# The last stage of a graph kernel: the addition of y moved from GpSimd to VectorE, in an order written out by hand

## The chip, the cores and the metric

The kernel runs on one core of one Trainium2 chip. A core has engines that run side by side, each with its own queue of instructions that it takes in order: TensorE (PE, matrix products into PSUM), VectorE (DVE), ScalarE (ACT), GpSimd (POOL), and SyncE (SP), whose queue issues most of the transfers between HBM and the on-chip memory SBUF. [...] The metric is the time of one execution on the device in microseconds (us), the median of several runs.

## The reference

A graph with 6250 nodes of 256 features and 100,000 edges, sorted by target node, goes through three relational layers, a residual layer norm, an attention of a special kind, and another residual layer norm:

```
for l in range(3):
    msg = (x @ W_rel[l, r])[edge_type, src]            # r = edge_type, 8 of them
    x = relu(segment_sum(msg, dst) + x @ W_root[l] + bias[l])
y = layernorm(x_in + x)
xt = (y @ weight).reshape(n, 4, 64)                    # 4 heads of 64
alpha = softmax(leaky_relu(<xt[src], attn_l> + <xt[dst], attn_r>), over heads)
tmp[i] = sum over h of alpha[i, h] * xt[dst[i], h]      # the first n edges only
out = layernorm(y + tmp repeated over the 4 heads)
```

The sum `tmp` of row i belongs to edge i, not to node i. As the edges are sorted by target, the targets of the first 6250 edges are a few nodes with small numbers (below 32 here), so `xt[dst]` takes rows of a small table.

## The kernel before, in words

The 6250 nodes make 49 tiles of 128 rows (`NT`), the last with 106. Function `fast` runs everything: the tables of the edges (`tables`), the three layers (`layer`), and then `attention`. The layers are by far the longest part, and the change leaves their code alone; they run under `tc.manual_schedule()`, which keeps the instructions of each engine in the order in which the program gives them. `attention` is called outside of it: there the framework puts the instructions of each engine into an order of its own, by its own estimates. In both cases the framework adds the waits that data and buffers ask for.

The last layer writes y, tile by tile, to HBM. `attention` (lines 889 to 1034) then works in these steps:

1. Tables: `ohd` (a one-hot of each edge's target, 32 wide), `mask`, and `v` and `v3`, the logits of the few nodes concerned; `yp` is cleared on GpSimd (L929). TensorE makes the logits (L938) and `xt` (L952), the transformed features of the small nodes, with the four heads stacked along the partitions.
2. Scores (L961 to L983): the 49 tiles are cut into nine parts of `G` = 6 tiles, the last of them with a single tile (tile 48, 106 rows). For each part TensorE selects logits with one-hot matrices into a PSUM buffer of pool `ps_1`, VectorE multiplies with the mask (`sel`), sums it (`s1`, `s2`), adds the two and adds `ga`, giving `sc`.
3. Softmax over the heads, for all tiles at once (`softmax`, L861 to L867): the weights `a`.
4. `bn` (L990 to L994): for each part VectorE multiplies `ohd` with `a`: for each edge 4 x 32 numbers that are a head's weight at the target's place and zero elsewhere.
5. The parts (L996 to L1033), one after the other in program order. SP loads six tiles of y (`yg`, 768 KB, four buffers). TensorE turns `bn` (L1005, PSUM pool `ps_2`, two buffers), ScalarE copies it out (`bt`, L1007), TensorE multiplies it with `xt` (L1010, `po` in pool `ps_3`), ScalarE copies the product out (`td`, L1012), GpSimd adds y to it, repeating the 64 numbers for the four heads (`z`, L1014, two buffers). Then the layer norm: VectorE takes statistics (L1024, L1025), ScalarE the root (`rs`, L1026), VectorE the reciprocal and the offset (`rs` L1027, `nb` L1028), ScalarE applies them tile by tile (`o`, L1032), and SP stores `o` (`store`: L853 for full tiles, L856 for the 106 rows of the last tile).

The parts run in the order of `parts[1:] + parts[:1]`: the single tile is the eighth, and the last is the part with tiles 0 to 5. The exponential and the root are in different tables of ScalarE, so a table is loaded before the exponential and another before the first root (both appear in the trace as ACT_TABLE_LOAD).

Of the kernel before, what the change touches and what calls it, by code (L numbers as in the profile page):

```python
# [20 lines left out]
P = 128  # L21
# [137 lines left out]
def fast(tc, const, pl, x, xs, src, dst, edge_type, w_rel, w_root, bias, weight,  # L159
# [10 lines left out]
    with ExitStack() as top:  # L170
        tab = top.enter_context(tc.tile_pool(name="tab", bufs=1))
        ident = tab.tile([P, P], F32, name="ident")
        idx = tab.tile([P, CH * P], I32, name="idx")
        key = tab.tile([P, CH * P], F32, name="key")
        pos = tab.tile([1, CH * P], I32, name="pos")
        iota_p = tab.tile([P, 1], F32, name="iota_p")
        eps = tab.tile([P, 1], F32, name="eps")
        bias_b = tab.tile([P, L, D], F32, name="bias_b")
        w1x = tab.tile([P, KC, D + 2 * H], F32, name="w1x")
        altab = tab.tile([P, NT, H], F32, name="altab")  # L180
        al3 = tab.tile([P, 3, NT, H], BF16, name="al3")
# [12 lines left out]

        dram = top.enter_context(tc.tile_pool(name="lanes", bufs=1, space=DRAM))
        lane = dram.tile([NT * P], I32, name="lane")
        with tc.tile_pool(name="ps_p", bufs=2, space=PSUM) as ps_p:
            tables(tc, pl, ps_p, src, dst, edge_type, ident, idx, key, pos, iota, iota_p,
                   lane, hk, hl, hif, dt, flag, R, H)
        y = dram.tile([NT * P, D], F32, name="y")  # L200

        with ExitStack() as s:
            wp = s.enter_context(tc.tile_pool(name="wp", bufs=1))
            sp = s.enter_context(tc.tile_pool(name="sp", bufs=1))
            mp = s.enter_context(tc.tile_pool(name="mp", bufs=8))
# [12 lines left out]
            nc.vector.memset(eps, EPS)  # L218
            for t in S:
                nc.scalar.memzero(t)  # L220
            nc.sync.dma_start(bias_b, bias.rearrange("l d -> (l d)").partition_broadcast(P))
            fold_weights(tc, mp, w1x, weight, attn_l, attn_r)

            def load_w(l):
                wr = wp.tile([P, KC, R, D], F32, name="wr")
                wo = wp.tile([P, KC, D], F32, name="wo")
                for k in range(KC):
                    nc.scalar.dma_start(
                        wr[:, k], w_rel[l, :, k * P:(k + 1) * P, :].rearrange("r p e -> p r e"))
                    nc.scalar.dma_start(wo[:, k], w_root[l, k * P:(k + 1) * P, :])  # L230
                return wr, wo

            groups = pl.order()

            ready = {}
            for i, (f, g) in enumerate(groups):
                for j in pl.reach(g):
                    ready[f, j] = i

            with tc.manual_schedule():  # L240
                for l in range(L):
                    wr, wo = load_w(l)
                    opn = layer(
                        tc, pl, l, l == L - 1, groups, ready, S, hold, A, hk, hl, idx, key, pos,
                        iota, ident, wr, wo, bias_b, x, xs, eps, w1x, altab, y,
                        (al3, ga, hif, yT0, lane, dst, iota_p),
                        mp, op, xp, hp, ps_w, ps_d, ps_t, H)

        attention(tc, pl, opn, A, al3, ga, hif, dt, yT0, iota, ident, eps, w1x, altab, y, out, H)


def tables(tc, pl, ps_t, src, dst, edge_type, ident, idx, key, pos, iota, iota_p, lane, hk, hl,
# [634 lines left out]
def attention(tc, pl, opn, A, al3, ga, hif, dt, yT0, iota, ident, eps, w1x, altab, y, out, H):  # L887
# [13 lines left out]
    with ExitStack() as s:  # L901
        q1 = s.enter_context(tc.tile_pool(name="q1", bufs=1))
        q2 = s.enter_context(tc.tile_pool(name="q2", bufs=2))
        q3 = s.enter_context(tc.tile_pool(name="q3", bufs=4))
        ps_1 = s.enter_context(tc.tile_pool(name="ps_1", bufs=3, space=PSUM))
        ps_2 = s.enter_context(tc.tile_pool(name="ps_2", bufs=2, space=PSUM))
        ps_3 = s.enter_context(tc.tile_pool(name="ps_3", bufs=2, space=PSUM))
        low, high = halves(A)

        parts = [range(a, min(a + G, NT)) for a in range(0, NT, G)]  # L910
        parts = parts[1:] + parts[:1]

        def rows_of(js):
            t = q3.tile([P, G, D], F32, name="yg")
            nc.sync.dma_start(t[:, :len(js)], y[js[0] * P:(js[-1] + 1) * P, :].rearrange(
                "(t p) d -> p t d", p=P))
            return t


        ohd = q1.tile([P, NT, DB], F32, name="ohd")  # L920
# [36 lines left out]


        sc = q1.tile([P, NT, H], F32, name="sc")
        C = NL * 3 * H  # L960
        for js in parts:  # L961
            g, e = len(js), slice(js[0], js[-1] + 1)
            pg = ps_1.tile([P, 512], F32, name="p1")
            for u, t in enumerate(js):
# [7 lines left out]
            nc.vector.tensor_tensor(  # L972
                sel[:, :g], pg[:, :g * C].rearrange("p (t n q) -> p t n q", t=g, n=NL),
                mask[:, e].unsqueeze(3).to_broadcast([P, g, NL, 3 * H]), ALU.mult)
            s1 = q2.tile([P, G, H], F32, name="s1")
            s2 = q2.tile([P, G, H], F32, name="s2")
            nc.vector.tensor_reduce(s1[:, :g], sel[:, :g].rearrange("p t n (c h) -> p t h (n c)", h=H),
                                    AX.X, ALU.add)
            nc.vector.tensor_reduce(
                s2[:, :g], pg[:, G * C:G * C + g * 3 * H].rearrange("p (t c h) -> p t h c", t=g, h=H),  # L980
                AX.X, ALU.add)
            nc.vector.tensor_tensor(s1[:, :g], s1[:, :g], s2[:, :g], ALU.add)
            nc.vector.tensor_tensor(sc[:, e], s1[:, :g], ga[:, e], ALU.add)  # L983
        a = q1.tile([P, NT, H], F32, name="a")
        m = q1.tile([P, NT], F32, name="m")
        softmax(nc, a, sc, m, NT, H)


        bn = q1.tile([P, NT, H, DB], F32, name="bn")
        for js in parts:  # L990
            g, e = len(js), slice(js[0], js[-1] + 1)
            nc.vector.tensor_tensor(  # L992
                bn[:, e], ohd[:, e].unsqueeze(2).to_broadcast([P, g, H, DB]),
                a[:, e].unsqueeze(3).to_broadcast([P, g, H, DB]), ALU.mult)  # L994

        for js in parts:  # L996
            g, e = len(js), slice(js[0], js[-1] + 1)
            yg = rows_of(js)

            bt = q2.tile([P, G, P], F32, name="bt")  # L1000
            for u0 in range(0, g, 4):
                n = min(4, g - u0)
# [5 lines left out]
            po = ps_3.tile([P, 512], F32, name="p3")  # L1008
            for u in range(g):
                nc.tensor.matmul(po[:, u * DH:(u + 1) * DH], bt[:, u], xt, start=True, stop=True)  # L1010
            td = q2.tile([P, G, DH], F32, name="td")
            nc.scalar.copy(td[:, :g].rearrange("p g d -> p (g d)"), po[:, :g * DH])  # L1012
            z = q2.tile([P, G, D], F32, name="z")
            nc.gpsimd.tensor_tensor(  # L1014
                z[:, :g].rearrange("p g (h d) -> p g h d", h=H),
                yg[:, :g].rearrange("p g (h d) -> p g h d", h=H),
                td[:, :g].unsqueeze(2).to_broadcast([P, g, H, DH]), ALU.add)

            st = q2.tile([P, G, 6], F32, name="st")
            mv = q2.tile([P, G, 2], F32, name="mv")  # L1020
            rs = q2.tile([P, G], F32, name="rs")
            nb = q2.tile([P, G], F32, name="nb")
            for t in range(g):
                nc.vector.bn_stats(st[:, t], z[:, t])  # L1024
                nc.vector.bn_aggr(mv[:, t], st[:, t])  # L1025
            nc.scalar.activation(rs[:, :g], mv[:, :g, 1], AF.Sqrt, bias=eps)  # L1026
            nc.vector.reciprocal(rs[:, :g], rs[:, :g])  # L1027
            nc.vector.scalar_tensor_tensor(nb[:, :g], mv[:, :g, 0], -1.0, rs[:, :g],  # L1028
                                           op0=ALU.mult, op1=ALU.mult)
            o = q2.tile([P, G, D], F32, name="o")  # L1030
            for t in range(g):
                nc.scalar.activation(o[:, t], z[:, t], AF.Identity, bias=nb[:, t:t + 1],  # L1032
                                     scale=rs[:, t:t + 1])  # L1033
            store(nc, out, o, js[0], g)


def general(tc, x, src, dst, edge_type, w_rel, w_root, bias, weight, attn_l, attn_r, out):
# [295 lines left out]
```

## Time and profile before

| | |
|---|---|
| median of 3 runs | 2999.32 us (2997.8 to 3003.55) |
| profiled execution, its own time | 2994.72 us |
| its span, first to last instruction | 2993.0 us |
| granted TensorE clock, mean of the span | 0.933 |
| granted TensorE clock from 2893 us on | 0.50 |
| first instruction of the attention | 2892.68 us |
| softmax done, `bn` begins | 2915.56 us |
| last norm issued / last store issued | 2985.77 / 2986.38 us |

Busy in the whole span: PE 2667.7 us (89%), DVE 1667.6 (56%), ACT 462.6 (15%), POOL 2159.9 (72%). These shares are those of the layers. In the last 71 us, from 2915.5 to 2986.4, TensorE is busy for 34.1 us, VectorE for 43.0, ScalarE for 38.3 and GpSimd for 29.3.

In the views, L1014 is line 1014 of the kernel before; `z<-yg,td` names what an instruction writes and reads; `x8` counts instructions; PEld is TensorE's loading of weights. In a timeline the first number is the start and the second the duration in us, and brackets give the idle time before an instruction and what ended it; neighbouring instructions of one kind are merged into one row. A table of waits gives the total in us, the number of times, and the longest. A group of instructions gives busy time, the mean of one in ns, and the idle time just before them with what ended it. In a stretch, each engine has its busy time and the number of its instructions, and at the end stand the granted clock, the busy share of the sixteen DMA engines and GB/s.

### The profile page before, as it was taken

To read this page: it belongs to the slowest core of one execution; us is meant where nothing else is said; L and a number is where in the kernel's file an instruction comes from. 1 tells how busy PE (TensorE), PEld (TensorE's weight loads), DVE (VectorE), ACT (ScalarE), POOL (GpSimd) and SP (SyncE) were. 2 spreads that over 40 slices of the span, in tenths; PEclk is the share of its full clock that TensorE was granted. 3 is DMA by queue.
4 is the path that set the end of the run, shared out by engine and by line. 5 is a ranking of instruction groups with operands and counts; after the bars stand their busy time and mean duration, and the time that the engine had idled before them with its cause. 6 is when DMAs were issued, how large, how long until landed. Compare 5 with 4: busy or idle time off the path is not lost. (4 is left out here: it accounts for less than half of the span.)

```text
span 2993.0 us, 45318 instructions
## 1 busy us (share of the span) xinstructions
PE 2667.7 (89%) x15710; PEld 2424.1 (81%) x15711; DVE 1667.6 (56%) x4106; ACT 462.6 (15%) x611; POOL 2159.9 (72%) x2258
## 2 busy tenths in 40 slices
PE   5999999999987799999998997789999999999874
PEld 4989888888876798998887887678888888898763
DVE  7655667754433555554444443355656655555775
ACT  2111111111001111111111010011111111111015
POOL 6777777777775777777777777577777777777723
PEclk9999999999878899999999997799999999999885
DMA  5444444445433344444434543344444444454634
GB/s 153 125 123 122 119 123 120 120 133 170 135 116 115 117 123 122 125 123 118 123 116 146 164 126 117 117 119 131 126 132 128 125 127 127 150 169 138 187 97 131
DMA packets 203053, 388.97 MB, mean 130 GB/s; under 512 B 42885, under 2 KB 128004, under 8 KB 202820
## 3 DMA queue, kind: packets, MB, share of 16 engines
q0 software_dynamic: 107424, 293.48, 33.7%
q1 hardware_dynamic: 87464, 85.04, 8.9%
q10 hardware_dynamic: 7932, 7.48, 0.7%
q8 instruction: 130, 2.13, 0.3%
q14 instruction: 103, 0.84, 0.1%
HBM read 360.18 MB, written 25.65 MB: 129 GB/s over the span
## 5 line engine op out<-in xcount | busy, mean ns | idle before, releaser
L496 POOL DMA_INDIRECT msg<-x,idx x1492 | 1419.2, 951 | 504.6 <-issue 411.9
L513 PE MATMUL pw<-oh,msg 128*128 128x160 f32 (+22 forms) x8952 | 1308.0, 303 | 195.6 <-DMA msg<-x,idx 101.4
L513 PEld LDWEIGHTS pw<-oh,msg 128*128 128x128 f32 x8952 | 1253.8, 202 | 261.2 <-issue 119.9
L525 DVE TENSOR_TENSOR S<-S,pw 128x320 f32 (+22 forms) x2238 | 904.5, 404 | 989.4 <-PE pd L581 508.1
L581 PE MATMUL pd<-wr,S 128*128 128x256 f32 x4704 | 1107.0, 385 | 1.7 <-DVE S L525 1.4
L581 PEld LDWEIGHTS pd<-wr,S 128*128 128x128 f32 x4704 | 893.1, 193 | 119.3 <-DVE S L525 3.6
L496 POOL DMA_INDIRECT msg<-in_x_dram,idx x746 | 709.0, 950 | 236.0 <-issue 210.8
L480 DVE TENSOR_TENSOR oh<-iota,key 128x640 f32<-128x640 f32 (+23 forms) x564 | 363.8, 647 | 26.4 <-issue 14.8
L590 ACT ACTIVATE S<-S 128x2048 uint32<-128x2048 uint32 x150 | 285.0, 1900 | 0.1
L551 ACT COPY xT<-pt 128x256 f32<-128x256 f32 x195 | 72.3, 371 | 972.6 <-PE pt L548 972.5
L598 ACT ACTIVATE h<-pd 128x256 f32<-128x256 f32 x98 | 37.7, 384 | 937.0 <-DVE pd L595 752.3
L577 PE MATMUL pd<-wo,xT 128*128 128x256 f32 x588 | 168.3, 412 | 3.3 <-ACT h L598 3.3
L595 DVE TENSOR_TENSOR pd<-pd,bias_b 128x256 f32<-128x256 f32 x147 | 63.1, 429 | 172.4 <-PE pd L581 172.3
L577 PEld LDWEIGHTS pd<-wo,xT 128*128 128x128 f32 x588 | 110.0, 205 | 13.1 <-ACT h L598 3.7
L647 DVE TENSOR_SCALAR sel<-iota,hk 128x392 bf16<-128x392 f32 x138 | 80.4, 613 | 0.0
L612 ACT ACTIVATE rs<-mv,eps 128x1 f32<-128x1 f32 x49 | 14.4, 295 | 413.1 <-DVE mv L611 413.1
L685 PE MATMUL pd<-msg,A 128*128 128x256 f32 x294 | 71.5, 386 | 1.5 <-DMA msg<-x 1.5
L1014 POOL TENSOR_TENSOR z<-yg,td 128x1536 f32<-128x1536 f32 (+1 forms) x9 | 29.3, 3268 | 56.7 <-DVE bn L992 28.0
L685 PEld LDWEIGHTS pd<-msg,A 128*128 128x128 f32 x294 | 55.7, 196 | 8.5 <-issue 1.8
L548 PE MATMUL pt<-ident,xin 128*128 128x128 f32 x294 | 57.4, 278 | 1.4 <-ACT xT L551 1.4
L629 PEld LDWEIGHTS pt<-w1x,xT 128*128 128x128 f32 x192 | 25.8, 195 | 35.2 <-ACT xT L551 35.2
L548 PEld LDWEIGHTS pt<-ident,xin 128*128 128x128 f32 x294 | 41.2, 145 | 12.7 <-ACT xT L551 2.4
(187 smaller groups left out, 669.4 us busy)
## 6 DMA issues: line engine op xcount, KB each, us to landing
msg<-x,idx POOLq DMA_INDIRECT x1492, 2.7
x<-h SPq DMA_DIRECT2D x96, 128.0 KB
xin<-x SPq DMA_DIRECT2D x96, 128.0 KB
msg<-x SPq DMA_DIRECT2D x24, 512.0 KB
msg<-in_x_dram,idx POOLq DMA_INDIRECT x746, 2.7
y<-yt SPq DMA_DIRECT2D x49, 128.0 KB
wr<-in_L_gnn_W_rel_dram ACTq DMA_DIRECT2D x6, 1024.0 KB
xin<-in_x_dram SPq DMA_DIRECT2D x48, 128.0 KB
```

The lines of the kernel that those rows point to most:

```text
L480: nc.vector.tensor_tensor(oh[:, :len(g), :w], iota[:, :w].unsqueeze(1).to_broadcast([P, len(g), w]), key[:, g[0]:g[-1] + 1].unsqueeze(2).t ...
L496: nc.gpsimd.indirect_dma_start(out=msg[:, q, :], out_offset=None, in_=table, in_offset=bass.IndirectOffsetOnAxis(ap=idx[:, t:t + 1], axis=0))
L513: nc.tensor.matmul(pw[:, k * w:(k + 1) * w], msg[:, q, k * P:(k + 1) * P], oh[:, q, :w], start=True, stop=True)
L525: ins = nc.vector.tensor_tensor(o, o, pw.rearrange("p (a b) -> p a b", b=W), ALU.add)
L548: nc.tensor.transpose(pt[:, k * P:(k + 1) * P], t[:, k * P:(k + 1) * P], ident)
L551: nc.scalar.copy(xT.rearrange("p k n -> p (k n)"), pt[:, :D])
L577: nc.tensor.matmul(pd[:, :D], xT[:, k], wo[:, k], start=(k == 0), stop=False)
L581: i = nc.tensor.matmul(pd[:, :D], s[:, k * R + r], wr[:, k, r], start=False, stop=(k == KC - 1 and r == R - 1))
L590: i = nc.scalar.memzero(cols(f, j))
L595: nc.vector.tensor_tensor(pd[:, :D], pd[:, :D], bias_b[:, l], ALU.add)
L647: nc.vector.tensor_scalar(oh, iota[:, :NT * R], float(512 * n), hk[:, t:t + 1], op0=ALU.add, op1=ALU.is_equal)
L685: nc.tensor.matmul(ph[:, :D], A[:, j], t[:, n], start=(n == 0), stop=(j == js[-1]))
```

## The change

- `attention` is now called under `tc.manual_schedule()`: the order on each engine is the program's.
- The first three loads of y are issued at the head of the attention, and each later one two parts further ahead in program order (part c + 3 after the addition of part c).
- The scores' PSUM pool has two buffers instead of three. `s1` and `s2` are tiles for all 49 tiles, and the two additions that give `sc` are made once, after the loop.
- `bn`: the first four parts stay on VectorE, the other five go to GpSimd.
- The part loop is cut into functions. `td` is gone: VectorE adds y to the product in PSUM (`summed`). z has four buffers (pool `q3`) instead of two. The six statistics come ahead of the six aggregations. The functions are called so that the products of part c + 1 come ahead of the addition of part c, and the norms of part c - 1 after the statistics of part c.
- The part order puts tiles 0 to 5 eighth and the single tile last.

The norms (`o`) were on ScalarE before and stay there.

```diff
+        with tc.manual_schedule():
+            attention(tc, pl, opn, A, al3, ga, hif, dt, yT0, iota, ident, eps, w1x, altab, y, out, H)
...
-        ps_1 = s.enter_context(tc.tile_pool(name="ps_1", bufs=3, space=PSUM))
+        ps_1 = s.enter_context(tc.tile_pool(name="ps_1", bufs=2, space=PSUM))
...
-        parts = parts[1:] + parts[:1]
+        parts = parts[1:-1] + parts[:1] + parts[-1:]
...
+        ygs = {c: rows_of(parts[c]) for c in range(3)}
...
+        s1 = q1.tile([P, NT, H], F32, name="s1")
+        s2 = q1.tile([P, NT, H], F32, name="s2")
...
-            nc.vector.tensor_tensor(s1[:, :g], s1[:, :g], s2[:, :g], ALU.add)
-            nc.vector.tensor_tensor(sc[:, e], s1[:, :g], ga[:, e], ALU.add)
+        nc.vector.tensor_tensor(sc, s1, s2, ALU.add)
+        nc.vector.tensor_tensor(sc, sc, ga, ALU.add)
...
-        for js in parts:
+        for c, js in enumerate(parts):
             g, e = len(js), slice(js[0], js[-1] + 1)
-            nc.vector.tensor_tensor(
+            (nc.vector if c < 4 else nc.gpsimd).tensor_tensor(
                 bn[:, e], ohd[:, e].unsqueeze(2).to_broadcast([P, g, H, DB]),
                 a[:, e].unsqueeze(3).to_broadcast([P, g, H, DB]), ALU.mult)
-        for js in parts:
-            g, e = len(js), slice(js[0], js[-1] + 1)
-            yg = rows_of(js)
+        def weighted(js):
...
             po = ps_3.tile([P, 512], F32, name="p3")
             for u in range(g):
                 nc.tensor.matmul(po[:, u * DH:(u + 1) * DH], bt[:, u], xt, start=True, stop=True)
-            td = q2.tile([P, G, DH], F32, name="td")
-            nc.scalar.copy(td[:, :g].rearrange("p g d -> p (g d)"), po[:, :g * DH])
-            z = q2.tile([P, G, D], F32, name="z")
-            nc.gpsimd.tensor_tensor(
+            return po
+
+        def summed(js, po, yg):
+            g = len(js)
+            z = q3.tile([P, G, D], F32, name="z")
+            nc.vector.tensor_tensor(
                 z[:, :g].rearrange("p g (h d) -> p g h d", h=H),
                 yg[:, :g].rearrange("p g (h d) -> p g h d", h=H),
-                td[:, :g].unsqueeze(2).to_broadcast([P, g, H, DH]), ALU.add)
+                po[:, :g * DH].rearrange("p (g d) -> p g d", d=DH).unsqueeze(2)
+                .to_broadcast([P, g, H, DH]), ALU.add)
+            return z
+
+        def measured(js, z):
...
             for t in range(g):
                 nc.vector.bn_stats(st[:, t], z[:, t])
+            for t in range(g):
                 nc.vector.bn_aggr(mv[:, t], st[:, t])
-            nc.scalar.activation(rs[:, :g], mv[:, :g, 1], AF.Sqrt, bias=eps)
+            return mv
+
+        def rooted(js, mv):
+            rs = q2.tile([P, G], F32, name="rs")
+            nc.scalar.activation(rs[:, :len(js)], mv[:, :len(js), 1], AF.Sqrt, bias=eps)
+            return rs
+
+        def scaled(js, mv, rs):
...
+        def normed(js, z, rs, nb):
...
+        n = len(parts)
+        pos = {0: weighted(parts[0])}
+        prev = None
+        for c in range(n + 1):
+            if c + 1 < n:
+                pos[c + 1] = weighted(parts[c + 1])
+            if c < n:
+                z = summed(parts[c], pos.pop(c), ygs.pop(c))
+                if c + 3 < n:
+                    ygs[c + 3] = rows_of(parts[c + 3])
+            if prev:
+                js, pz_, mv_, rs_ = prev
+                nb = scaled(js, mv_, rs_)
+            if c < n:
+                mv = measured(parts[c], z)
+            if prev:
+                normed(js, pz_, rs_, nb)
+            prev = (parts[c], z, mv, rooted(parts[c], mv)) if c < n else None
```

`scaled` holds the reciprocal and `nb` (L1027, L1028 of before), `normed` the six norms and the store.

More of the change, by code (lines that the diff above doesn't have):

```diff
@@ L247, in fast @@
                         mp, op, xp, hp, ps_w, ps_d, ps_t, H)
-        attention(tc, pl, opn, A, al3, ga, hif, dt, yT0, iota, ident, eps, w1x, altab, y, out, H)
+        with tc.manual_schedule():
+            attention(tc, pl, opn, A, al3, ga, hif, dt, yT0, iota, ident, eps, w1x, altab, y, out, H)
 def tables(tc, pl, ps_t, src, dst, edge_type, ident, idx, key, pos, iota, iota_p, lane, hk, hl,
@@ L974, in attention @@
                 mask[:, e].unsqueeze(3).to_broadcast([P, g, NL, 3 * H]), ALU.mult)
-            s1 = q2.tile([P, G, H], F32, name="s1")
-            s2 = q2.tile([P, G, H], F32, name="s2")
-            nc.vector.tensor_reduce(s1[:, :g], sel[:, :g].rearrange("p t n (c h) -> p t h (n c)", h=H),
+            nc.vector.tensor_reduce(s1[:, e], sel[:, :g].rearrange("p t n (c h) -> p t h (n c)", h=H),
                                     AX.X, ALU.add)
             nc.vector.tensor_reduce(
-                s2[:, :g], pg[:, G * C:G * C + g * 3 * H].rearrange("p (t c h) -> p t h c", t=g, h=H),
+                s2[:, e], pg[:, G * C:G * C + g * 3 * H].rearrange("p (t c h) -> p t h c", t=g, h=H),
                 AX.X, ALU.add)
-            nc.vector.tensor_tensor(s1[:, :g], s1[:, :g], s2[:, :g], ALU.add)
-            nc.vector.tensor_tensor(sc[:, e], s1[:, :g], ga[:, e], ALU.add)
+        nc.vector.tensor_tensor(sc, s1, s2, ALU.add)
+        nc.vector.tensor_tensor(sc, sc, ga, ALU.add)
         a = q1.tile([P, NT, H], F32, name="a")
@@ L1010, in attention @@
                 nc.tensor.matmul(po[:, u * DH:(u + 1) * DH], bt[:, u], xt, start=True, stop=True)
-            td = q2.tile([P, G, DH], F32, name="td")
-            nc.scalar.copy(td[:, :g].rearrange("p g d -> p (g d)"), po[:, :g * DH])
-            z = q2.tile([P, G, D], F32, name="z")
-            nc.gpsimd.tensor_tensor(
+            return po
+        def summed(js, po, yg):
+            g = len(js)
+            z = q3.tile([P, G, D], F32, name="z")
+            nc.vector.tensor_tensor(
                 z[:, :g].rearrange("p g (h d) -> p g h d", h=H),
                 yg[:, :g].rearrange("p g (h d) -> p g h d", h=H),
-                td[:, :g].unsqueeze(2).to_broadcast([P, g, H, DH]), ALU.add)
+                po[:, :g * DH].rearrange("p (g d) -> p g d", d=DH).unsqueeze(2)
+                .to_broadcast([P, g, H, DH]), ALU.add)
+            return z
+        def measured(js, z):
+            g = len(js)
             st = q2.tile([P, G, 6], F32, name="st")
             mv = q2.tile([P, G, 2], F32, name="mv")
-            rs = q2.tile([P, G], F32, name="rs")
-            nb = q2.tile([P, G], F32, name="nb")
             for t in range(g):
                 nc.vector.bn_stats(st[:, t], z[:, t])
+            for t in range(g):
                 nc.vector.bn_aggr(mv[:, t], st[:, t])
-            nc.scalar.activation(rs[:, :g], mv[:, :g, 1], AF.Sqrt, bias=eps)
+            return mv
[4 more added lines that the diff above has]
+        def scaled(js, mv, rs):
+            g = len(js)
+            nb = q2.tile([P, G], F32, name="nb")
             nc.vector.reciprocal(rs[:, :g], rs[:, :g])
@@ L1029, in attention @@
                                            op0=ALU.mult, op1=ALU.mult)
+            return nb
+        def normed(js, z, rs, nb):
+            g = len(js)
             o = q2.tile([P, G, D], F32, name="o")
```

## The prediction

> **What bounds the kernel now.** I read the page's totals first: they describe the three graph layers (2892 of 2993 us), which the change doesn't touch. So I took the chain of waits of the last stretch, the timeline there, the waits by engine, and the same stretch cut at its rounds. The attention begins at 2892.68; its scores and softmax end at 2915.52; the nine parts run from there to the last norm at 2986.36.
>
> One round of the parts in the timeline (start, duration, engine, line):
>
> ```profile
> 2951.32 3.49 POOL L1014 TENSOR_TENSOR z<-yg,td 128x1536 f32<-128x1536 f32 x1 [4.14 <-ACT o L1032]
> ...
> 2951.64 3.20 DVE L1028 SCALAR_TENSOR_TENSOR nb<-mv,rs 128x6 f32<-128x6 f32 x1
> ...
> 2954.87 3.06 ACT L1032 ACTIVATE o<-z,nb,rs 128x256 f32<-128x256 f32 x6 [2.65 <-DVE nb L1028]
> ...
> 2957.83 0.28 ACT L1026 ACTIVATE rs<-mv,eps 128x6 f32<-128x6 f32 x1
> ...
> 2958.06 3.51 POOL L1014 TENSOR_TENSOR z<-yg,td 128x1536 f32<-128x1536 f32 x1 [3.25 <-ACT o L1032]
> ```
>
> z has two buffers, so GpSimd's next add waits for the six norms (3.06) that free one; the tiny nb, 0.17 us elsewhere, then stands 3.20 us until that add ends, and the next norms need nb. Add, norms, add: 3.49 + 3.06 + 0.19 of hand-over = 6.74 us a round, in turn instead of side by side. The waits from 2915 on say the same:
>
> ```profile
> POOL z L1014 <- ACT o L1032: 25.1, 5, 10.7
> ...
> DVE rs L1027 <- ACT rs L1026: 12.4, 8, 4.3
> DVE st L1024 <- POOL z L1014: 12.0, 5, 6.1
> ...
> ACT o L1032 <- DVE nb L1028: 7.8, 5, 2.6
> ACT o L1032 <- POOL z L1014: 6.6, 2, 3.5
> ```
>
> The second loss is the start: the first z are done at 2926.2 and 2929.6, yet the first root comes at 2936.24, as the order put it behind four parts' copies.
>
> ```profile
> 2934.94 1.28 ACT L1026 ACT_TABLE_LOAD   x1
> 2936.24 0.30 ACT L1026 ACTIVATE rs<-mv,eps 128x6 f32<-128x6 f32 x1
> ```
>
> The stretches (PE, weight load, DVE, ACT, POOL busy; clock; DMA) show no engine full; no engine is the bound, the taking of turns is:
>
> ```profile
> 2951.30:2958.10 6.80, 2.19 (x9) 1.89 (x9) 5.92 (x14) 4.15 (x11) 3.53 (x2) 0.50 0.60 186
> ```
>
> Of DVE's 5.92 there, 3.2 is the standing nb. The third loss is small: the last part is a full one, so six norms (3.06) and a 768 KB store end the program:
>
> ```profile
> 2983.30 3.06 ACT L1032 ACTIVATE o<-z,nb,rs 128x256 f32<-128x256 f32 x6 [0.51 <-DVE nb L1028]
> 2986.38 0.38 SPq L853 DMA_DIRECT2D out_dram<-o  x1
> ```
>
> [...] nb (two SBUF inputs) agrees: 3.15 to 3.21 us beside an add, 0.17 without; so do the one-input statistics, 0.39 us in both cases. A VectorE add with one input in PSUM beside a GpSimd operation is not in this trace. [...]
>
> **The change by parts**, with durations from these rows:
>
> ```profile
> L1010 PE MATMUL p<-xt,bt 128*128 128x64 f32 x98 | 23.6, 425 | 18.0 <-ACT bt L1007 18.0
> ...
> L1024 DVE BATCH_NORM_STATS2 st<-z 128x6 f32<-128x256 f32 x49 | 19.1, 402 | 12.0 <-POOL z L1014 12.0
> ...
> L1025 DVE BATCH_NORM_AGGREGATE mv<-st 128x2 f32<-128x6 f32 x49 | 7.8, 167 | 0.0
> L992 DVE TENSOR_TENSOR bn<-ohd,a 128x768 f32<-128x768 f32 x8 | 7.1, 951 | 0.0
> L1007 ACT COPY bt<-p 128x512 f32<-128x512 f32 x8 | 4.7, 582 | 4.7 <-PE p L1005 4.7
> L1012 ACT COPY td<-p 128x384 f32<-128x384 f32 x8 | 3.8, 470 | 11.4 <-PE p L1010 11.4
> ```
>
> *Scores.* Before: 14.28 us (first sel 2898.37, last sc 2912.65), 1.67 a part. The two small adds leave each part (about 0.09 of pitch each), but in program order s1 follows sel directly and waits its whole 0.63; then 0.83 and 0.14: 1.60 a part. Eight of these, about 0.6 for the single tile, and two adds of 128x196 (0.36 + 0.04 each, as in the softmax): 14.2. I take 0. Two PSUM buffers instead of three: refilling takes PE about 1.0, inside the 1.60. The three early y loads head SP's queue as the first four do now: 0. Softmax: same.
>
> *bn.* VectorE keeps four (0.87 start to start, done at 2919.04), GpSimd gets four full ones and the single tile. Price not in the trace; from z, 3.49/1536 = 2.27 ns an element, 768 take 1.75 and 128 some 0.4: 7.4 us. [...] They are needed when TensorE turns part 4, near 2934.6, eight us after their end; that cover hides them. But both engines start from the same softmax, with two SBUF inputs each. Ends: 0 (VectorE's four run through), or each VectorE product waits for one of GpSimd's: three times 1.75, 5.2 less the 2.1 of slack before VectorE is needed again at 2921.2, so +3.2; all of GpSimd's first would be 7.4 - 2.1 = +5.3. I take 0: VectorE made `a` itself and follows 0.04 later. A gain isn't excluded by that, but the transposes already start on the first product: none.
>
> *Part 0* stays on the trace's own times: transposes 2916.57, its product done 2921.2, td's old start 2921.22. The td copies (0.47 on ScalarE) and GpSimd's z go. New is VectorE's z add, 1536 elements, one input in PSUM. Nearest rows: ohd, 1568 elements from SBUF, 1.79; sel, 432 from PSUM, 0.60, at about 1 ns for each element more 1.70. So 1.70; ends 1.6 and 2.5 (a slow repeat in PSUM, nothing like it seen). Then statistics 6 x 0.31 + 0.1 and aggregates 6 x 0.08 + 0.1: 2.5. z is ready 2922.9, mv 2925.45. The root's table load falls after part 1's copies (2922.95) while ScalarE waits: hidden; without that wait 1.3. First root done at 2925.8, 10.7 earlier than the 2936.5 of before.
>
> *Steady state*, from T, a root's end. VectorE per part: add 1.70, reciprocal and nb 0.42, statistics 2.5: 4.62. ScalarE: two bt copies 0.95, six norms 3.06, root 0.30: 4.31 and hand-overs. TensorE: transposes 1.49 and products 2.82: 4.31. Walked through in the written order: copies to T + 0.95; products of the next part to T + 3.5; norms from T + 1.3 (nb comes behind the current add) to T + 4.35; root to T + 4.65. VectorE comes out at the same length, 4.65. Round 1 is longer, since VectorE and ScalarE start together: the add of part 1 waits for its product (2925.6), nb comes at 2927.75, norms to 2930.85, root 2931.15. Six rounds of 4.65 then put part 7's root at 2959.1.
>
> *Loads and stores.* SP issues load c+3, then store c-1, which waits for norms; the next load queues behind it but is wanted two rounds later. A part is 1.57 MB in and out, at the 312 to 369 GB/s of the last store some 4.7 us, but four loads are early; some 4.2 parts of loads and 8.2 of stores are left, 9.7 MB in 39 us, 29 of them needed: hidden.
>
> *End.* Part 7's norms end at 2962.7, the single tile's root 2963.0, scale 2963.45, its norm 2964.1. The 106 KB store isn't small in time: before it was issued at 2980.55 and moved data from about 2981.3 to 2985.1, at a DMA share near 0.12[...]. Put last, it stands partly behind part 7's store (data to about 2966): done at 2969 to 2970, and from the last data (2990.3) to the span's end were 2.7: 2972.2. So the smallest part last saves norms, but gives back about 2.8 us in its store (a full one at 2962.75 would end the span 6.6 later, at 2969.4).
>
> **Sum.** 2993.0 - 2972.2 = 20.8 us. Made of 10.7 (the first root earlier), 11.5 (from the first root to the last norm 49.8 before, 38.3 after) and -1.4 (from there to the span's end 6.6 before, 8.1 after). The profiled execution took 2994.72, 1.72 around its span: 2973.9. The median of the runs is 4.60 above it, so 2999.3 - 20.8 = 2978.5; I say 2978.
>
> **Rivals.**
> - [...] GpSimd's products hold up VectorE (bn, then nb of part 0, one 1.75 more): +3.2 to +7, about 2983. For: both start at once[...]. Against: it happens once, before the rounds.
> - *The written order paces it*: root, copies, products, add, statistics of one part make a loop over two rounds of about 0.3 + 0.95 + 2.9 + 1.7 + 0.45 + 2.5 + hand-overs = 9.1, 4.6 a round; there is no reserve. With 0.1 more at each of eight hand-overs a round is 5.5, seven rounds +6: 2984.
> - *Slower*: the PSUM add with its repeated operand runs far below rate and VectorE becomes the bound. It decides at 20.8/8.2 = 2.5 us over 1.70, 4.2 an add; at 5.2 the kernel is 7 us slower, 3006. Against: sel takes 0.60 for 432 from PSUM, 1.4 ns an element with its fixed part.
> - *No difference*: written order loses at other places what turns cost now: 2999. It would need rounds of 7.2, against busy sums of 4.3 to 4.6.
>
> **How the numbers follow.** Likeliest case 0.62, 2978 (its own range 2973 to 2982); [...] order 0.10; no difference 0.03; slower 0.03. Runs before spread by 5.75 us, so 0.2% (6 us) is about what can be told from none. The first three are all faster by more than that: 0.94; same 0.03; slower 0.03. 2972 to 2986 holds the likeliest case and most of the two rivals beyond it.
>
> **What would show it.** Right: GpSimd idle after about 2927, no nb above 0.3 us, adds of 1.7, roots every 4.65, first root near 2925.8, last activation near 2964, eight us to the end with little DMA in the last ones. Wrong: bn rows on VectorE of 2 to 3 us (quarrel); VectorE waiting for TensorE or ScalarE for bt in most rounds (order); adds over 2.5.

## The result and the profile after

The changed kernel takes 2977.94 us (median of 4 runs, 2973.59 to 2982.89), the kernel before 3000.55 us (4 runs, 2997.8 to 3003.55): a ratio of 0.9925, with a 95% interval of 0.9905 to 0.9945. That is 22.6 us less; the forecast was 2978. (The median of before is 1.2 us above the one that the forecast started from, as a fourth run came in.)

The profiled execution of the changed kernel took 2982.89 us, with a span of 2981.1. Its attention starts at 2902.93, 10.25 us later than in the profile of before (2892.68). This difference lies in the layers, whose code is the same, and comes with the run: the medians differ by 22.6 us, the two profiled spans by only 11.9. So the attention's own length, from the first `ohd` to the span's end, is compared from here on: 100.32 us before, 78.17 after, 22.15 less. It divides so ("norm" is the application of the layer norm, L1032 of before; the forecast's column is the prediction's own sum):

| stretch of the attention | before | after | difference | forecast |
|---|---|---|---|---|
| first `ohd` to first `bn` | 22.88 | 22.84 | 0.0 | 0 |
| first `bn` to the end of the first root | 20.98 | 11.92 | -9.1 | -10.7 |
| first root to the end of the last norm | 49.82 | 35.95 | -13.9 | -11.5 |
| last norm to the span's end | 6.64 | 7.46 | +0.8 | +1.4 |
| sum | 100.32 | 78.17 | -22.15 | -20.8 |

A round is the time from one addition of y to the next. One round of the changed kernel in the timeline, in order of start (start, duration, engine, line):

```profile
2949.89 0.50 DVE L1032 BATCH_NORM_AGGREGATE mv<-st 128x2 f32<-128x6 f32 x6
2950.30 1.75 DVE L1018 TENSOR_TENSOR z<-yg,p 128x1536 f32<-128x1536 f32 x1
...
2951.01 0.28 ACT L1037 ACTIVATE rs<-mv,eps 128x6 f32<-128x6 f32 x1
2951.20 0.82 ACT L1009 COPY bt<-p 128x512 f32<-128x512 f32 x2
...
2951.97 0.18 DVE L1043 RECIPROCAL rs<-rs 128x6 f32<-128x6 f32 x1
2952.19 0.17 DVE L1044 SCALAR_TENSOR_TENSOR nb<-mv,rs 128x6 f32<-128x6 f32 x1
2952.27 2.05 DVE L1030 BATCH_NORM_STATS2 st<-z 128x6 f32<-128x256 f32 x6
2952.39 3.06 ACT L1053 ACTIVATE o<-z,nb,rs 128x256 f32<-128x256 f32 x6 [0.36 <-DVE nb L1044]
2954.24 0.49 DVE L1032 BATCH_NORM_AGGREGATE mv<-st 128x2 f32<-128x6 f32 x6
```

VectorE has no gap: add, reciprocal, nb, statistics, aggregates, next add. The norms run beside the statistics of the next part, and nb takes 0.17 us instead of 3.20. The stretch of that round (PE, weight load, DVE, ACT, POOL busy; clock; DMA share; GB/s):

```profile
2951.30:2955.65 4.35, 4.08 (x20) 3.70 (x18) 4.32 (x16) 3.99 (x10) 0.00 (x0) 0.50 1.04 341
```

VectorE is busy for 4.32 of 4.35 us: it is the bound now. TensorE and ScalarE are close behind. So is DMA, whose share reads 1.04 here; but in the whole attention VectorE has no wait that the profile puts down to a load of y, so the loads don't set the pace. In the waits from 2880 on, nothing of the old ties is left; the norms wait 8 times for nb, 4.2 us in all, and once for a store:

```profile
ACT o L1053 <- DVE nb L1044: 4.2, 8, 1.1
...
ACT o L1053 <- DMA out_dram<-o: 0.6, 1, 0.6
```

One thing goes against the likeliest case of the forecast, the `bn` products at the start, on VectorE and on GpSimd:

```profile
2925.77 7.42 DVE L995 TENSOR_TENSOR bn<-ohd,a 128x768 f32<-128x768 f32 x4
2933.11 1.74 DVE L1018 TENSOR_TENSOR z<-yg,p 128x1536 f32<-128x1536 f32 x1
```
```profile
2925.82 9.06 POOL L995 TENSOR_TENSOR bn<-ohd,a 128x768 f32<-128x768 f32 x5 [21.81 <-DVE a L868]
```

Four products on VectorE take 7.42 us instead of 3.56. Seen one by one they start at 2925.77, 2926.65, 2928.81 and 2930.96; GpSimd's first three end at 2928.07, 2930.22 and 2932.37. From the second on, both engines advance by one product each in 2.16 us: they take strict turns.

### The profile page after: what moved, and what is told of

Read it like the earlier page. It is cut to its first block, busy times and chain, and to the rows that moved or that the text cites. A ratio compares the mean times of both kernels' runs of the same rounds, so it can differ in the third digit from the quotient of the medians.

```text
span 2981.1 us, 45287 instructions
## 1 busy us (share of the span) xinstructions
PE 2671.0 (90%) x15710; PEld 2428.2 (81%) x15711; DVE 1668.5 (56%) x4094; ACT 458.6 (15%) x602; POOL 2140.4 (72%) x2254
## 4 chain that ended last, share of the span: by engine, by line
PE 69%; POOL 10%; issue 8%; DVE 6%; DMA 5%; ACT 2%; DVEq 0%; ACTq 0%; POOLq 0%; SPq 0%
PE pw L514 31%; PE pd L582 29%; POOL msg L497 10%; PE pd L578 4%; DMA msg<-x,idx 3%; DVE S L526 3%; PE pd L686 1%; DMA msg<-in_x_dram,idx 1%; PE pt L549 1%; PE pt L630 1%; ACT xT L552 1%; PE pd L657 1%; ACT o L1053 0%; DMA wr<-in_L_gnn_W_rel_dram 0%; DVE oh L481 0%
## 5 line engine op out<-in xcount | busy, mean ns | idle before, releaser
L630 PE MATMUL pt<-w1x,xT 128*128 128x4 f32 x192 | 30.8, 266 | 23.5 <-ACT xT L552 23.5
```

Of the source, the lines that this page charges most:

```text
L630: nc.tensor.matmul(pt[:, :H], yT[:, k], w1x[:, k, D + H:D + 2 * H], start=(k == 0), stop=(k == KC - 1))
```

## The experiments

In the experiments the layers were much slower, in every kernel and the one before too: it took 3630.27, 3621.92 and, in the last set, a median of 3656.11 us. The attention was not: its stretch to the first `bn` takes 22.84 us there too in most of these kernels, and the changed kernel's whole attention 77.98 (78.17 in its first profile). So the attention's length is what is compared, and the whole time is given only where a kernel was run several times. Each length is that of one profile. The two profiles of the changed kernel differ by 0.19 us, so a few tenths say nothing; the attention of the kernel before was profiled once, 100.32.

**Four z buffers, nothing else** (on the kernel before).

```diff
-            z = q2.tile([P, G, D], F32, name="z")
+            z = q2.tile([P, G, D], F32, name="z", bufs=4)
```

> The kernel before with four z buffers instead of two, nothing else. The measure in all these runs is the attention's own length in the profile, from the first ohd to the span's end (100.3 us before, 78.2 in the changed kernel), as the layers ahead vary by several us from one execution to the next. My theory: rounds of 6.74 us are GpSimd's add and the norms taking turns[...]. With four buffers the add no longer waits for norms; nb still stands up to 3.2 us a part. Rounds near 5.9 (VectorE: 2.5 statistics + 0.2 + 3.2), attention 93 to 96. Rival, the buffers alone are the tie: rounds of 4.8, attention near 87. [...]

Measured: attention 94.85, 5.5 less, so nb's wait is not the only tie (that would have left 100). This is inside the range of my theory, but not by its way. Even rounds of 5.9, set by a standing nb, did not come: from the third part on the additions of full parts start between 4.4 and 10.4 us apart, and the framework's order for this kernel twice puts the norms of two parts in a row. nb still stands in places, and the norms wait for stores as well, 6.0 us in two waits that the kernel before doesn't have:

```profile
3578.57 2.53 DVE L1028 SCALAR_TENSOR_TENSOR nb<-mv,rs 128x6 f32<-128x6 f32 x1
```
```profile
ACT o L1032 <- DMA out_dram<-o: 6.0, 2, 3.5
```

The buffers are one of the ties, and not the only one. How much of the rest is nb, the stores or the new order, this run alone does not separate.

**nb with one input in PSUM** (on the kernel before).

```diff
...
-            nc.vector.reciprocal(rs[:, :g], rs[:, :g])
-            nc.vector.scalar_tensor_tensor(nb[:, :g], mv[:, :g, 0], -1.0, rs[:, :g],
+            pr = ps_r.tile([P, 512], F32, name="pr")
+            nc.vector.reciprocal(pr[:, :g], rs[:, :g])
+            nc.vector.tensor_copy(rs[:, :g], pr[:, :g])
+            nc.vector.scalar_tensor_tensor(nb[:, :g], mv[:, :g, 0], -1.0, pr[:, :g],
```

> The kernel before, where the reciprocal goes to PSUM (and is copied back for the norms), so that nb has one input in SBUF and one in PSUM; z stays on GpSimd with two buffers. Scores get two PSUM buffers instead of three to make room. My theory: nb falls from 3.2 to about 0.2 us beside an add, the norms of a part run beside the next add, rounds fall from 6.74 to about 4.9, attention 86 to 89. Rival, the two z buffers are the tie: nb short but rounds stay at 6.5 or more, attention 98 to 100. [...]

Measured: attention 95.98, 4.3 less, between the two ranges. The first part of the theory holds: nb is short with an add running beside it:

```profile
3584.76 3.45 POOL L1015 TENSOR_TENSOR z<-yg,td 128x1536 f32<-128x1536 f32 x1 [3.82 <-ACT o L1035]
...
3585.17 0.15 DVE L1031 SCALAR_TENSOR_TENSOR nb<-mv,pr 128x6 f32<-128x6 f32 x1
...
3585.56 3.06 ACT L1035 ACTIVATE o<-z,nb,rs 128x256 f32<-128x256 f32 x6
```

nb takes 0.15 instead of 3.2. The size was wrong: adds start at 3584.76 and, two parts on, at 3595.31, 10.55 later, so 5.3 a round and not 4.9. With two buffers an add also has to wait for the whole life of the z two parts back: its add 3.45, statistics 2.6, root and nb 0.9, norms 3.06 make 10.0, over two buffers 5.0 and hand-overs. So each tie taken away alone is worth some 4 to 6 us, and neither is the whole. Both together were not taken from the kernel before.

**The changed kernel, order left to the framework.** The line `with tc.manual_schedule():` becomes `if True:`, nothing else.

> The changed kernel without the order by hand in the attention. If the hand order gives the early first root (10.7 us of the 22), the first root comes again 8 to 11 us later than with it and the attention is 86 to 90. Rival, the removal of GpSimd's add from the rounds is everything: attention 77 to 80.

Measured: attention 86.20, 8.0 more than with the order and at the low end of the forecast. The first root starts 17.24 us after the first `bn` instead of 11.62, again behind copies of later parts:

```profile
3557.34 0.58 ACT L1009 COPY bt<-p 128x512 f32<-128x512 f32 x1 [3.54 <-PE p L1007]
3557.94 1.28 ACT L1037 ACT_TABLE_LOAD   x1
3559.24 0.30 ACT L1037 ACTIVATE rs<-mv,eps 128x6 f32<-128x6 f32 x1
```

That is 5.6 us later, and not the 8 to 11 of the forecast. The stretches behind it are 3.5 us longer, and the one ahead of `bn` is 1.0 us shorter in the framework's order (21.80 against 22.84). So of the 22 us, 14 come without the hand order and 8 with it, if the order is the last thing added.

**The addition back on GpSimd, hand order kept.**

```diff
-            nc.vector.tensor_tensor(
+            td = q2.tile([P, G, DH], F32, name="td")
+            nc.scalar.copy(td[:, :g].rearrange("p g d -> p (g d)"), po[:, :g * DH])
+            nc.gpsimd.tensor_tensor(
...
-                po[:, :g * DH].rearrange("p (g d) -> p g d", d=DH).unsqueeze(2)
-                .to_broadcast([P, g, H, DH]), ALU.add)
+                td[:, :g].unsqueeze(2).to_broadcast([P, g, H, DH]), ALU.add)
```

> The changed kernel with the addition of y back on GpSimd (and the td copy on ScalarE ahead of it), four z buffers and the hand order kept. My theory: nb again waits for an add (3.2 us where one runs), and an add of 3.5 instead of 1.7 stands between product and statistics; rounds of 5.5 to 6.5, attention 86 to 94. Rival, order and buffers alone bring the gain: attention 78 to 80.

Measured: attention 103.28, more than before the change, and outside both ranges. My reason fell with it, since in the full rounds nb never stands (it does once, 0.72, beside the single tile's addition):

```profile
3591.39 3.44 POOL L1020 TENSOR_TENSOR z<-yg,td 128x1536 f32<-128x1536 f32 x1 [4.16 <-ACT td L1019]
...
3594.86 2.06 DVE L1031 BATCH_NORM_STATS2 st<-z 128x6 f32<-128x256 f32 x6 [4.31 <-POOL z L1020]
...
3597.43 0.30 ACT L1038 ACTIVATE rs<-mv,eps 128x6 f32<-128x6 f32 x1 [3.23 <-DVE mv L1033]
...
3597.99 0.17 DVE L1045 SCALAR_TENSOR_TENSOR nb<-mv,rs 128x6 f32<-128x6 f32 x1
3598.36 0.49 ACT L1019 COPY td<-p 128x384 f32<-128x384 f32 x1
...
3598.99 3.44 POOL L1020 TENSOR_TENSOR z<-yg,td 128x1536 f32<-128x1536 f32 x1 [4.16 <-ACT td L1019]
```

The round is a single loop of 7.60: add, statistics, root, copies, td, next add. In this order td stands on ScalarE behind the root of the part before, and the add waits for td. This left open whether GpSimd or the place of td costs the 25 us.

**GpSimd's addition in an order made for it.** As the last, with the products two parts ahead and td and the addition one part ahead of the statistics. The lines that move the addition are those of the last cut and are left out here.

```diff
-        pos = {0: weighted(parts[0])}
+        pos = {c: weighted(parts[c]) for c in range(2)}
+        zs = {0: summed(parts[0], pos.pop(0), ygs.pop(0))}
...
+            if c + 2 < n:
+                pos[c + 2] = weighted(parts[c + 2])
             if c + 1 < n:
-                pos[c + 1] = weighted(parts[c + 1])
+                zs[c + 1] = summed(parts[c + 1], pos.pop(c + 1), ygs.pop(c + 1))
             if c < n:
-                z = summed(parts[c], pos.pop(c), ygs.pop(c))
+                z = zs.pop(c)
```

> The addition of y on GpSimd (td copy on ScalarE ahead of it, four z buffers) in a hand order made for it: products two parts ahead, td copy and addition one part ahead of the statistics. If the 25 us between the GpSimd addition in the other hand order and the changed kernel came from the place of td behind root and copies, and not from GpSimd's speed, the rounds fall from 7.55 to ScalarE's sum, 0.95 + 0.47 + 3.06 + 0.3 = 4.8, and the attention is 80 to 84. [...]

Measured: attention 80.28, rounds of 4.35 to 4.4 (adds at 3585.41, 3589.76, 3594.12), as short as with VectorE's add, and not over 6, as they were expected if GpSimd's add (3.44 us) set the pace. The place of td and of the addition in the order was 23 of the 25 us. What is left between the two kernels, 2.1 to 2.3 (80.28 against 78.17 and 77.98), lies at the start, where the first root comes 15.04 us after the first `bn` instead of 11.62. Two things stand there: GpSimd's first addition starts only at 3573.43, when its own five `bn` products are done, and it takes 3.4 us instead of 1.74. With GpSimd's products elsewhere it was not run.

The rounds are as short for another reason than in the changed kernel. The stretch of one of them (columns as above):

```profile
3589.76:3594.12 4.36, 4.11 (x20) 3.71 (x20) 2.83 (x15) 4.36 (x11) 3.45 (x2) 0.50 1.02 330
```

VectorE, rid of the addition, is busy for only 2.83 us; ScalarE, with the td copy, is busy for all 4.36 and is the bound, as this run's expectation had it (its sum of 4.8 was too long). So moving the addition only exchanges one bound of 4.36 us for another.

In the full rounds nb takes 0.17, since it ends before the next add starts. Only where the last two adds run one after the other does it stand, 0.66.

**The kernel before under the hand order alone,** its program order kept.

```diff
-        attention(tc, pl, opn, A, al3, ga, hif, dt, yT0, iota, ident, eps, w1x, altab, y, out, H)
+        with tc.manual_schedule():
+            attention(tc, pl, opn, A, al3, ga, hif, dt, yT0, iota, ident, eps, w1x, altab, y, out, H)
```

> The kernel before under the hand order alone, its program order kept: each part's copies, product, td, addition, statistics, root and norms one after the other. A part's chain is 0.95 + 2.8 + 0.5 + 3.5 + 2.5 + 0.3 + 0.4 + 3.1 = 14 us with nothing of the next part beside it on ScalarE: attention 135 to 150, slower than before by 35 to 50. Rival, the framework's order was the loss and any order by hand mends it: under 95.

Measured: attention 181.59, 81 us more than before; the direction was right, the size too small. Rounds take 17.5 us instead of 14. The first root does come earlier, 13.86 us after the first `bn` instead of 20.68, but the rounds lose far more. The term I had left out is in what the add waits for:

```profile
3682.52 3.42 POOL L1015 TENSOR_TENSOR z<-yg,td 128x1536 f32<-128x1536 f32 x1 [14.06 <-DMA yg<-y]
```

In program order the load of y stands on SP behind the store of the part before, which waits for that part's norms, so the load's own time comes into the loop (issued at 3676.23 in this round, 6.3 us before the add; a part later the norms end at 3693.20, the store is issued at 3693.23 and the load at 3693.70). Another 3.1 us lie in the scores, where in program order the two small additions wait in each part: 2.05 us a part instead of 1.67. An order by hand is not a gain by itself; what counts is which order. That the early loads of y are a part of it is read from this wait; they were not tried alone.

**All bn products on VectorE** (on the changed kernel).

```diff
-            (nc.vector if c < 4 else nc.gpsimd).tensor_tensor(
+            nc.vector.tensor_tensor(
```

> The changed kernel with all nine bn products on VectorE. In the changed kernel's trace VectorE and GpSimd take strict turns over bn, 2.16 us for a pair, so VectorE reaches the first addition of y 7.34 us after bn began. My theory: nine products at 0.87 on VectorE alone also end at 7.3, so GpSimd's help buys nothing: first addition at 7.2 to 7.6, attention 77.5 to 79. Rival, GpSimd does relieve VectorE: attention over 80.

Measured: attention 77.81, inside the range of my theory. Nine products end as early as four that take turns:

```profile
3526.93 7.24 DVE L995 TENSOR_TENSOR bn<-ohd,a 128x768 f32<-128x768 f32 x9
3534.09 1.75 DVE L1018 TENSOR_TENSOR z<-yg,p 128x1536 f32<-128x1536 f32 x1
```

The first addition comes 7.16 us after the first product, 7.34 in the changed kernel. GpSimd's five products bought nothing.

**GpSimd's products after VectorE's four** (on the changed kernel).

```diff
+        turn = q1.tile([P, 1], F32, name="turn")
...
+            if c == 4:
+                nc.gpsimd.tensor_copy(turn, bn[:, parts[3][-1], 0, 0:1])
```

> The changed kernel where GpSimd first copies one number of VectorE's fourth bn product and so starts its own five after VectorE's four. My theory: no turns any more, VectorE's four end 3.5 us after bn began, the first addition comes when its product is ready (5.6 to 5.8), 1.7 earlier, attention 76 to 77. Rival, the products of part 4 come too late or nb of part 0 meets a GpSimd product, up to 1.4 us: attention 77.5 to 79.

Measured: attention 77.06, just outside the range of 76 to 77. The turns are gone, and so is the delay:

```profile
3541.78 3.56 DVE L998 TENSOR_TENSOR bn<-ohd,a 128x768 f32<-128x768 f32 x4
3547.44 1.75 DVE L1021 TENSOR_TENSOR z<-yg,p 128x1536 f32<-128x1536 f32 x1 [2.10 <-PE p L1015]
```
```profile
3545.56 6.14 POOL L998 TENSOR_TENSOR bn<-ohd,a 128x768 f32<-128x768 f32 x5
```

The addition starts 5.66 us after the first product, the first root 9.95 us after it, 1.67 earlier than in the changed kernel. The last norm keeps 1.5 of it, the end 1.1, as the tail is 0.4 longer here (7.87).

**The last store cut at 96 rows** (on the changed kernel).

```diff
-        nc.sync.dma_start(out[(j0 + full) * P:N, :], o[:last, full])
+        cut = last - last % 16
+        nc.sync.dma_start(out[(j0 + full) * P:(j0 + full) * P + cut, :], o[:cut, full])
+        if cut < last:
+            nc.sync.dma_start(out[(j0 + full) * P + cut:N, :], o[cut:last, full])
```

> The changed kernel with the last store, 106 rows, issued as 96 and 10 rows. My theory: [...] the last data moves about 2.5 us sooner, from the last norm to the span's end 4.5 to 5.5 us instead of 7.46, attention 75 to 76.5. Rival, the time is the fixed cost of a store at the end: 7 to 8 us as before, attention 78.

Measured: attention 77.11; from the last norm to the end 6.59 us instead of 7.46, so 0.9 less, and not the 2 to 3 of my theory: between the two forecasts. The data does move sooner. A stretch of the changed kernel, when part 7's store is over, and below it the stretch of the run with the cut that stands at the same place:

```profile
2976.00:2976.50 0.50, 0.00 (x0) 0.00 (x0) 0.00 (x0) 0.00 (x0) 0.00 (x0) 0.50 0.12 39
```
```profile
3591.50:3592.00 0.50, 0.00 (x0) 0.00 (x0) 0.00 (x0) 0.00 (x0) 0.00 (x0) 0.50 0.10 10
```

In the changed kernel the DMA engines go on at shares of 0.05 to 0.25 until 2979.5, 5.9 after the last norm's end; with the cut, the stores' data stops at about 3592.5, 3.4 after it. But the end follows 1.6 later in the one and 3.2 in the other. What the last 3 us after a store hold, the traces don't show. Why the store of 106 rows is slow they don't show either; measured is its share, near 0.12, and that its data is done sooner when it is cut into 96 and 10 rows.

**A full part last** (on the changed kernel).

```diff
-        parts = parts[1:-1] + parts[:1] + parts[-1:]
+        parts = parts[1:] + parts[:1]
```

> The changed kernel with the part order of before: the single tile eighth, a full part last. My theory: the smallest part last saves the norms but pays in its slow store, so the order of the parts is worth nothing as it stands: attention 77.5 to 79.5. Rival, the smallest part last is worth its norms, 2.5 us and more: attention 80.5 to 82.

Measured: attention 80.23, 2.1 us more than in the changed kernel, between my two ranges. The tail is shorter (6.75 instead of 7.46), the last norm ends 2.4 us later (50.30 instead of 47.87 after the first `bn`), and the scores, which follow the same order of parts, take 0.3 us more. The small part eighth doesn't fill a round, and the full part behind it waits for its products:

```profile
3591.63 1.75 DVE L1018 TENSOR_TENSOR z<-yg,p 128x1536 f32<-128x1536 f32 x1 [2.40 <-PE p L1012]
```

So the smallest part last is worth 2 us.

**The changed kernel again, and with both small improvements,** each run several times beside the kernel before.

> The changed kernel once more, as it is, on this chip: attention 77.5 to 78.5, as in its first profile; the whole 22 us under the kernel before, whatever the layers take on this chip.

> The changed kernel with both small improvements: GpSimd's bn products after VectorE's four, and the last store cut into 96 and 10 rows. Each alone gave 1.1 us of the attention; they lie in different places, so 75.5 to 76.5 of attention, 2 us under the changed kernel and 24 under the kernel before. Rival: they overlap somewhere and give 77.

Measured: the changed kernel, attention 77.98; time 3630.51 against 3656.11, ratio 0.9926 (0.9903 to 0.9949). That is 6 runs against 11. With both improvements, attention 76.34, as expected; time 3630.70 (7 runs), ratio 0.9926 (0.9905 to 0.9947). The 1.6 us show in the profile, but can't be told from none in the whole time: single runs of the second kernel reach from 3607.28 to 3657.57. The gain of the change itself, 25.6 us in this set, agrees with the first comparison within the intervals, though the layers take some 650 us more.

## Why the prediction was right

The time, 2977.94, was forecast as 2978, and the attention lost 22.15 us where 20.8 were summed. The steps, one by one:

- **What bounds it** (add and norms in turn, tied by two z buffers and by nb, which stands until GpSimd's add ends, 3.15 to 3.21 us): shown in the main. Each tie taken away alone gives 5.5 and 4.3 us, the first under an order that changed with it; nb falls to 0.15 beside an add once one input lies in PSUM. With four buffers and nb clear of the adds, GpSimd still adding, the rounds are 4.36.
- **The late first root,** put down to the framework's order: shown twice. Without the hand order the changed kernel's first root is 5.6 us later, and with the hand order alone that of the kernel before is 6.8 us earlier. Neither is the whole of the 9.1.
- **Scores at nothing:** right, 22.84 against 22.88; a part takes 1.61, as worked out.
- **bn at nothing:** wrong. The rival that GpSimd's products hold up VectorE, given 0.22, did happen. VectorE reached the first addition 7.34 us after the first product, 1.69 later than the 5.65 taken from the trace of before. My end of +3.2 had the mechanism (turns of one product each) and too high a price: 2.27 ns an element from z made 1.75 for a GpSimd product; alone it takes 1.47, or 1.9 ns an element, so the measurement lies below the 2.27 from z. With 0.88 for VectorE's first product and three turns of 2.16, the end comes at 7.36. The reason given for taking none, that VectorE made `a` itself and so comes first, holds for the first product only.
- **The addition at 1.70:** right, 1.72 to 1.75. That it isn't held by a GpSimd operation, which the trace of before could not show, is visible once: the first one, 1.74 at 2933.11, runs beside GpSimd's fourth product (2932.34 to 2934.53).
- **Rounds of 4.65:** too long, measured about 4.4, with 4.9 for the first instead of 5.35. The wrong terms are VectorE's: statistics and aggregates take about 2.4 from their start to the next addition (2.5 taken), reciprocal and nb 0.30 (0.42). The records overlap a little: the addition at 2954.67 starts before the aggregates' end at 2954.73. VectorE is the bound in the rounds, as forecast. This made up for the 1.7 lost at bn.
- **The written order sets the pace** (rival, 0.10): no. The rounds are as long as VectorE's own work; hand-overs added nothing. Its price in the forecast does not follow from its own loop either: eight hand-overs of 0.1 on 9.1 us over two rounds make 4.95 a round, not 5.5.
- **Loads and stores hidden:** right but for 0.6 us, where one norm waits for a store. At a share of 0.87 over the five rounds from 2942.6 on, DMA is nearer to being the bound than the 29 of 39 us that I worked out. An estimate from the prediction's 1.57 MB a part and 391 GB/s, the rate of the half microsecond from 2974.0 on: 4.0 us a round, not far under the 4.36.
- **Tail +1.4:** measured +0.8. The store of the 106 rows is slow as described (shares of 0.05 to 0.25 until 2979.5), but cutting it saves 0.9 us, not the 2.8 of the text; the small part last is still worth 2.1.
- **Slower** (rival, 0.03): no, as the addition takes 1.75. By its own terms an addition of 5.2 would have cost 7.9 us, not 7.

That 2978 was hit to a tenth of a microsecond is luck. Errors of opposite sign, +1.7 up to the first root and -2.0 in the rounds, nearly cancel, and with -0.9 behind them and -0.1 elsewhere the attention lost 1.35 us more than was summed; the median of before then came out 1.2 us higher than the forecast had it, which hides that. Single runs of a kernel spread by 6 to 9 us. The forecast of some 21 us less, by ending the turns and the late root, was right by its mechanism.

The forecast did not ask which of the edits carries the gain, and the title names the addition's engine first. The runs say: with GpSimd still adding, in an order made for it, the attention takes 80.28 us, so some 20 of the 22 us do not need the move. In the changed kernel's own order the same addition on GpSimd costs 25. The 20 us come from working ahead: more z buffers, products and additions ahead of the statistics, nb ahead of what could hold it, early loads, the small part last. Only the last of these was taken back alone in the new order, 2.1 us; how the others share the rest is not shown.

## What to carry to other kernels

When two engines work in turn, look for all the ties, here a buffer's whole life and an instruction that stands until the other engine's ends (nb, 3.20 us), and count what each alone is worth before moving work to another engine: here an order that works one part ahead brought the attention with GpSimd's slow addition (3.44 us) to within 2.3 us of that with VectorE's fast one (1.75), and the same addition in the wrong place of a hand order cost 25. After a change, look again for the bound: here VectorE with the addition and ScalarE with the td copy came to the same 4.36 us.

Splitting the `bn` products between VectorE and GpSimd bought nothing while both worked on them at the same time, each with two SBUF inputs (78.17 us against 77.81 with all on VectorE); one engine after the other was 1.1 us better. Cutting the last small store into 96 and 10 rows was worth 0.9 us. Both gains are below what the time of the whole kernel can show.

## What the runs showed of the hardware

- VectorE and GpSimd, each with a row of `bn` products of two SBUF inputs, took strict turns in the changed kernel: 2.16 us for a pair of products that take 0.95 (VectorE) and 1.47 (GpSimd) when VectorE's come first and GpSimd's after them. The ends alternate, VectorE's at 2926.73, 2928.88, 2931.04 and 2933.19, GpSimd's at 2928.07, 2930.22, 2932.37 and 2934.53: with products queued on both sides, neither engine finished two of its own in a row. What in the chip makes the turns is not shown.
- With one input in PSUM, VectorE was not held here: nb took 0.15 us beside an add on GpSimd, instead of 3.20 with both inputs in SBUF, and an addition of 128x1536 took 1.74 us beside a GpSimd product and 1.72 to 1.75 without.
- A store of 106 rows of 1 KB moved its data in about 3.8 us when alone (2981.3 to 2985.1 in the profile of before), longer than one of 768 rows (about 2987.1 to 2990.3).
